# Dense work of the third of four attention layers: a smaller budget per sub-step and a lower bar for a second piece

## The chip, the cores and the metric

The kernel runs on one core of a Trainium2 chip. A core has a matrix engine (TensorE, PE in the profile), whose weight loads are listed apart (PEld), a vector engine (VectorE, DVE), an engine for activations and copies (ScalarE, ACT), a general one (GpSimd, POOL), and a queue engine that here only issues transfers (SyncE, SP). The metric is the device time of one execution in microseconds (us); lower is better. The median of three executions of the kernel before is 1722.2 us (1716.13 to 1724.42).

## The reference

The input x has 8 batches of 256 tokens with 512 features, and there is a context of the same shape. Four cross-attention layers follow each other; each reads the output of the one before and the same context:

```python
x = layer1(x, ctx, mask)        # layer norm, 16 heads of 32, output projection, then an MLP 512 -> 2048 -> 512
x = layer2(x, ctx)              # one head of width 512: x + alpha * softmax(q k^T / sqrt(512)) v w_o
x = layer3(x, ctx, mask2)       # 32 query heads of 16 share 8 key/value heads; then layer norm
x = layer4(x, ctx, mask)        # 16 heads of 32 on the layer-normed context; x + tanh(gate) * out
```

For the third layer:

```python
scores = einsum('bkgld,bksd->bkgls', q, k) * scale + mask2   # per batch: 32 heads, 256 x 256
out    = einsum('bkgls,bksd->bkgld', softmax(scores), v) @ Wo + bo
y      = layer_norm(out + x) * gamma + beta
```

Everything is float32. The kernel reaches that accuracy by splitting a matrix into a rounded part ("hi") and a rest ("lo") and multiplying three times (hi hi, hi lo, lo hi), so a projection takes three times the matmuls that it would take once.

## The kernel before

**Stages.** First the attention of layer 1 with its own pipeline, then its MLP, then one pipeline (called at L1639) over 64 units: units 0 to 31 are layer 3, unit number 4b + ft for batch b and a quarter ft of the heads, and units 32 to 63 are layer 4. In the trace of before, layer 3's part runs from about 825 to 1416 us and layer 4's to the end.

**A tick.** Tick t of the pipeline has four sub-steps (chunks), written t.0 to t.3 here. In each, the attention of two units is issued first: A (L1277, scores of unit t with queries in rows, two matmuls; L1287, four VectorE instructions that add the mask and take the row maxima) and C (L1330, scores of unit t - 2 transposed, two matmuls; then L1340 copy on ScalarE and L1341 mask on GpSimd for the one half, L1343 on VectorE for the other, and L1345 the exponential on ScalarE). Once per tick come B (L1308 to L1311: the maxima of unit t - 1 are transposed and put, by a transfer, into the operand that C will use) and the product of probabilities and values, AV (L640), of the unit that has just ended C. AV's result goes through memory (avd, L1370 to L1375) and is divided in E (L1383 to L1388).

**The dense work as filler.** Everything else of layers 2 to 4 is written as generators that a class `Fillers` (L283) holds in a queue. After A and C of a sub-step the pipeline calls `tick(us, budget)` (L304). It adds the budget to an account, held to at most 8, and lets the generators advance piece by piece while the account is above zero; each piece takes its estimated time from it. So the account may go below zero by a large piece, and is filled again by the budgets that follow. For layer 3 the budget per sub-step is a quarter of B2 = 9.0, that is 2.25 (a quarter of 10 in the first three ticks); for layer 4 B3 = 5.5 holds.

**Who is next.** `one()` (L315) goes on first with a tile that is half done. Then it takes the first entry of the queue that has not run yet in this sub-step. An entry that has run may give a second piece only if the account is above 1.4:

```python
for again in (False, True):
    for e in self.q:
        if e[1] <= self.now and (not self.even or again and self.acc > 1.4 or e not in self.ran):
```

The entries are `l2_post` (L1544, ahead of the others), `l12_fill` (L1397: layer 2's attention and layer 3's queries, batch after batch) and `context_fill` (L1468: what is made of the context). `until()` (L339) forces pieces without regard to the account where the attention needs a result, and sets the account to zero.

**The pieces of a batch**, with the letters used below and the estimates that the account is charged:

| letter | piece | matmul line, tile | estimate, us |
|---|---|---|---|
| S | half a tile of the context times layer 2's key matrix (`scores_side` L1122) | L213 cx,ws | 1.28 |
| K | keys of layer 3 | L213 cx,ws | 1.28 |
| V | values of layer 3 | L227 ws,cx | 1.28 |
| R | half a tile of the context times layer 2's value matrix (`rows` L1165) | L227 ws,cx | 1.28 |
| X | layer 1's output transposed, two per batch (`features` L1185) | L1185 | 0.85 |
| s | half of layer 2's scores; behind the second the softmax, L1206 and L1207 on VectorE and L1211 twice on ScalarE | L1196 | 1.71 |
| T | transposes of those probabilities, copied by L1234 on ScalarE | L1228 | 0.85 |
| o | half of layer 2's output | L1241 | 1.71 |
| F | that output transposed, two per batch; copied out by L391 and its neighbours | L383 | 0.85 |
| Q | half of layer 3's queries | L213 x,wq | 1.28 |
| P | half a tile of the projection behind the attention (`l2_post`) | L227 wo,at | 1.28 |

A batch holds 18 of 1.28, four of 1.707 and five of 0.853, 34.1 in all.

**Order.** In ticks 2 to 25 the program order of TensorE is written out by hand (`keep_order` L776): A and C of a sub-step, then the sub-step's pieces; B and AV stand behind the first sub-step's pieces. From unit 26 on, the framework's scheduler sets the order. Transfers are issued by SyncE in one queue.

**Buffers.** The weights that S, K, V and R need come in through three slots `ws`: two for layer 2's key matrix (`med`), one for K and V (`wkvd`), and layer 2's value matrix (`mnd`, two loads of 1 MB issued where the last S ends) into the two slots that S has freed. The raw context of a batch is split into halves (L179 on ScalarE, L180 on GpSimd) some time ahead of the first S.

Of the kernel before, what the change touches and what calls it, by code (L numbers as in the profile page):

```python
# [20 lines left out]
PASSES = ((0, 0), (0, 1), (1, 0))  # L21
MMUS = 1.0 / 2400.0
B0, B0E = 6.2, 9.0
B2, B3 = 9.0, 5.5
LEAD = 5
N3, NFA = 0, 5
PRIO = 100
# [49 lines left out]
def tile_xattn_stack(  # L77
# [205 lines left out]
    class Fillers:  # L283
# [29 lines left out]
        def one(self):  # L313
            if self.open:
                self.adv(self.open)  # L315
                return True

            for again in (False, True):
                for e in self.q:
                    if e[1] <= self.now and (not self.even or again and self.acc > 1.4 or e not in self.ran):  # L320
                        self.ran.append(e)
                        self.adv(e)
                        return True
            return False
# [1255 lines left out]
    kst = [ph5.T([P, 4, 256], R, "ks") for _ in range(2)]  # L1580
    one = const.tile([4, 256], F, name="one")
    nc.gpsimd.memset(one, 1.0)
    for t in kst:
        nc.gpsimd.memset(fp(t), 0.0)
# [162 lines left out]
```

## Time and profile before

| quantity | value |
|---|---|
| median of three executions (range) | 1722.2 us (1716.13 to 1724.42) |
| the profiled execution, its time | 1719.88 us |
| its span, first to last instruction | 1718.1 us |
| mean granted TensorE clock | 0.968 of full speed |
| instructions | 28352 |
| moved by transfers | 329.16 MB, mean 192 GB/s |
| duration of ticks 16 to 19, one batch (1103.3 to 1167.5 us) | 64.2 us |

All durations below are from that one execution. A line of the page's group list names the source line, the engine, the operation, the output tile, an arrow and the input tiles, the shape, and how often; then busy time, the mean of one in ns, and the idle time of the engine ahead of the group with what ended most of it. A line of the waits reads: engine, waiting instruction, arrow, what released it; total idle time, how often, the longest. "Issue" is time in which nothing that the profile shows held the engine back. A line in order of time gives the start, the duration, the engine, the instruction, and in brackets the idle time ahead of it. The stretches give, between two times, the busy time of each engine, the mean granted clock of TensorE (PEclk; 1.00 is full speed), the share of time in which the transfer engines were busy, and GB/s.

### The profile page before, as it was taken

To read this page: it belongs to the slowest core of one execution; us is meant where nothing else is said; L and a number is where in the kernel's file an instruction comes from. 1 tells how busy PE (TensorE), PEld (TensorE's weight loads), DVE (VectorE), ACT (ScalarE), POOL (GpSimd) and SP (SyncE) were. 2 spreads that over 40 slices of the span, in tenths; PEclk is the share of its full clock that TensorE was granted. 3 is DMA by queue.
4 is the path that set the end of the run, shared out by engine and by line. 5 is a ranking of instruction groups with operands and counts; after the bars stand their busy time and mean duration, and the time that the engine had idled before them with its cause. 6 is when DMAs were issued, how large, how long until landed. Compare 5 with 4: busy or idle time off the path is not lost.

```text
span 1718.1 us, 28352 instructions
## 1 busy us (share of the span) xinstructions
PE 1591.8 (93%) x9984; PEld 1222.5 (71%) x9984; DVE 1071.7 (62%) x2380; ACT 875.8 (51%) x1563; POOL 774.5 (45%) x792
## 2 busy tenths in 40 slices
PE   6999999999989999999798899999988998999998
PEld 5877866777658778887576577677565876777765
DVE  7248556777756867643466578678777775654343
ACT  5226445555455565553255466565564564444454
POOL 6336234323474675532135456557556575222111
PEclk9999999999999999999899999999988999999999
DMA  8969677454542443356755575585366676766552
GB/s 290 306 225 304 205 234 229 153 167 130 179 159 81 151 131 126 120 188 217 238 186 199 168 272 178 192 278 170 107 192 187 200 224 201 231 215 212 179 164 74
DMA packets 169308, 329.16 MB, mean 192 GB/s; under 512 B 17200, under 2 KB 85200, under 8 KB 163664
## 3 DMA queue, kind: packets, MB, share of 16 engines
q1 hardware_dynamic: 169168, 327.36, 58.9%
q8 instruction: 80, 1.31, 0.3%
q14 instruction: 60, 0.49, 0.1%
HBM read 230.79 MB, written 96.49 MB: 190 GB/s over the span
## 4 chain that ended last, share of the span: by engine, by line
PE 60%; DMA 14%; DVE 10%; POOL 5%; issue 4%; ACT 3%; SPq 3%; DVEq 0%; POOLq 0%; ACTq 0%
PE pp L213 20%; PE pp L227 19%; PE av L640 7%; PE sm L1277 3%; PE sm L685 3%; PE st L721 3%; PE st L1330 2%; DVE sm L1287 2%; PE pp L1196 1%; PE pp L1241 1%; DMA h<-in_ctxn_dram 1%; PE pp L383 1%; DMA ws<-mnd 1%; DMA stack<-q0d 1%; POOL fw L180 1%
## 5 line engine op out<-in xcount | busy, mean ns | idle before, releaser
L692 DVE TENSOR_REDUCE negm<-sm 128x2 f32<-128x512 f32 x256 | 168.9, 682 | 126.1 <-PE sm L685 125.7
L729 ACT ACTIVATE P<-st 128x512 f32<-128x512 f32 x256 | 145.2, 594 | 125.3 <-PE st L721 118.3
L213 PE MATMUL pp<-ys,fw 128*128 128x512 f32 x768 | 190.2, 397 | 7.7 <-ACT fw L179 4.4
L227 PE MATMUL pp<-pw,gs 128*128 128x512 f32 x768 | 191.7, 396 | 2.9 <-ACT gs L1031 2.6
L213 PEld LDWEIGHTS pp<-ys,fw 128*128 128x128 f32 x768 | 143.2, 190 | 41.7 <-ACT fw L179 4.6
L640 PE MATMUL av<-P,V 128*32 128x256 f32 (+1 forms) x2204 | 168.8, 406 | 4.1 <-DVE xt L754 3.1
L227 PEld LDWEIGHTS pp<-pw,gs 128*128 128x128 f32 x768 | 141.1, 188 | 37.9 <-ACT gs L1031 3.7
L213 PE MATMUL pp<-x,wq 128*128 128x256 f32 x1152 | 159.4, 286 | 7.1 <-DVE x L391 2.2
L213 PEld LDWEIGHTS pp<-x,wq 128*128 128x128 f32 x1152 | 148.7, 190 | 16.6 <-DVE x L391 3.6
L1287 DVE CUSTOM_DVE_ANT_0 sm<-sm,va 128x256 f32<-128x256 f32 x256 | 103.6, 443 | 47.4 <-PE sm L1277 47.1
L1287 DVE CUSTOM_DVE_ANT_0 sm<-sm,vb 128x256 f32<-128x256 f32 x256 | 103.5, 442 | 47.2 <-PE sm L1277 46.9
L1032 POOL TENSOR_TENSOR gs<-xt,gs 128x512 fp32r<-128x512 f32 x64 | 91.9, 1443 | 85.6 <-ACT gs L1031 85.6
L1277 PE MATMUL sm<-ks,stack 96*128 96x512 f32 x256 | 100.3, 458 | 23.0 <-DVE mx L1287 12.6
L227 PE MATMUL pp<-wo,at 128*128 128x512 f32 x384 | 105.5, 408 | 4.5 <-POOL at L1387 1.7
L640 PEld LDWEIGHTS av<-P,V 128*32 128x32 f32 x2204 | 62.0, 110 | 60.0 <-issue 21.1
L1027 DVE SCALAR_TENSOR_TENSOR xt<-xt,xt 128x512 f32<-128x512 f32 x64 | 67.9, 1064 | 58.5 <-ACT xt L1026 58.5
L1345 ACT ACTIVATE P<-P 128x1024 f32<-128x1024 f32 x77 | 81.4, 1059 | 41.9 <-POOL P L1341 36.1
L180 POOL TENSOR_TENSOR fw<-stg,fw 128x1024 fp32r<-128x1024 f32 x32 | 82.2, 2578 | 34.5 <-ACT fw L179 19.5
L1277 PEld LDWEIGHTS sm<-ks,stack 96*128 96x128 f32 x256 | 46.8, 199 | 64.8 <-issue 52.8
L227 PEld LDWEIGHTS pp<-wo,at 128*128 128x128 f32 x384 | 70.2, 192 | 27.3 <-issue 3.3
L1330 PE MATMUL st<-stack,ks 100*128 100x512 f32 x256 | 87.2, 411 | 2.3 <-DVE P L1343 1.3
L697 POOL CAST mhl<-negm 128x8 fp32r<-128x8 f32 x64 | 16.1, 251 | 156.6 <-DVE negm L692 156.4
(215 smaller groups left out, 3613.5 us busy)
## 6 DMA issues: line engine op xcount, KB each, us to landing
stg<-in_wfc_dram SPq DMA_DIRECT2D x32, 512.0 KB
stg<-in_wpr_dram SPq DMA_DIRECT2D x32, 512.0 KB
ws<-med SPq DMA_DIRECT2D x16, 1024.0 KB
ws<-mnd SPq DMA_DIRECT2D x16, 1024.0 KB
q2d<-nat SPq DMA_DIRECT2D x48, 256.0 KB
stack<-q2d SPq DMA_DIRECT2D x32, 384.0 KB
k0d<-nat SPq DMA_DIRECT2D x16, 512.0 KB
stack<-k0d SPq DMA_DIRECT2D x32, 256.0 KB
```

The lines of the kernel that those rows point to most:

```text
L180: lo.tensor_tensor(w[:, 1], stg, fp(w[:, 0]), ALU.subtract)
L213: nc.tensor.matmul(pt[:, :n], lhsT=sel(ws, wj, kc)[:, ft * P : (ft + 1) * P], rhs=sel(xs, xj, kc), start=(k == 0), stop=(k == 11),)
L227: nc.tensor.matmul(pt[:, :n], lhsT=sel(xs, xj, kc)[:, tt * P : (tt + 1) * P], rhs=sel(ws, wj, kc), start=(k == 0), stop=(k == 11),)
L640: self.prev = nc.tensor.matmul(o, lhsT=lhsT, rhs=rhs, start=start, stop=stop, skip_group_check=True).ins
L692: nc.vector.tensor_reduce(self.negm[:, 2 * h : 2 * h + 2], pt.rearrange("p (q k) -> p q k", q=2), AX.X, ALU.max, negate=True)
L729: nc.scalar.activation(p, pt, AF.Exp)
L1027: nc.vector.scalar_tensor_tensor(v, v, 1.0 / GA, u, ALU.add, ALU.mult)
L1032: nc.gpsimd.tensor_tensor(lo, u, fp(hi), ALU.subtract)
L1277: nc.tensor.matmul(pts[qt], lhsT=self.qs[0:96, h, qt * P : (qt + 1) * P], rhs=self.ks[0:96].rearrange("p u k -> p (u k)"), start=True, sto ...
L1287: nc.vector.tensor_tensor_reduce(out=t, in0=t, in1=self.am[:, qt, :], scale=1.0, scalar=-3.0e38, op0=ALU.add, op1=ALU.max, accum_out=self. ...
L1330: nc.tensor.matmul(pt, lhsT=self.ks[0:100, u, kt * P : (kt + 1) * P], rhs=self.qs[0:100, 2 * hp : 2 * hp + 2, :].rearrange("p h t -> p (h ...
L1345: last["act"] = nc.scalar.activation(pf, pf, AF.Exp).ins
```

## The change

Two constants change. B2 falls from 9.0 to 8.6: the budget of a sub-step from 2.25 to 2.15, and of a batch's sixteen sub-steps from 36.0 to 34.4, against the 34.1 that a batch's pieces are charged. The bar for a second piece of the same entry in one sub-step falls from 1.4 to 0.9. The bar holds from the last stretch of the MLP on, B2 for units 3 to 31.

```diff
-B2, B3 = 9.0, 5.5
+B2, B3 = 8.6, 5.5
...
-                    if e[1] <= self.now and (not self.even or again and self.acc > 1.4 or e not in self.ran):
+                    if e[1] <= self.now and (not self.even or again and self.acc > 0.9 or e not in self.ran):
```

No instruction is added or taken away. What moves is the sub-step that a piece stands in. In a batch in the steady part (ticks 16 to 19; four sub-steps of a tick between bars):

| tick | before | after |
|---|---|---|
| 16 | T S, S, o S, S o | P P, s, s, T o |
| 17 | F, F K, Q Q, Q Q | o, F F, Q Q, Q Q |
| 18 | V, R R, R R, none | S S, S, S K, V |
| 19 | X, X s s, P P, P P | X R R, X R, R, P P |

So the sub-step 18.3 of each batch, without a piece before, has one after; 4.3 is empty in both. In tick 4 after, s and T of batch 1 stand together in 4.1. The first S of batch 3 moves from 5.2 to 6.0. In the tail, 25.1 to 26.0 were empty and now 26.0 to 26.3 are; before unit 32 starts, `until()` now forces five pieces of layer 4's dense work at once (two halves of a query or key projection, two of values, one transpose), and one small piece at 38.3. From unit 39 on the order of all engines is the same.

## The prediction

> **What bounds the kernel now.** I read the page first, then the stretches of the third layer, then TensorE's waits there, and at last single stretches in order of time.
>
> ```profile
> PE 1591.8 (93%) x9984; PEld 1222.5 (71%) x9984; DVE 1071.7 (62%) x2380; ACT 875.8 (51%) x1563; POOL 774.5 (45%) x792
> ...
> PE 60%; DMA 14%; DVE 10%; POOL 5%; issue 4%; ACT 3%; SPq 3%; DVEq 0%; POOLq 0%; ACTq 0%
> ```
>
> TensorE (PE) is busy 93% of the span and carries 60% of the chain that ended last. The change moves work on PE and adds none, so only PE's idle time, and the pace at which it runs, can change. Unit 3 chunk 3 to unit 26 (890.8 to 1270.0 us) is the part whose order changes most; "busy time by stretch" shows it whole, then one steady batch, then four short stretches of low granted clock:
>
> ```profile
> core 0: us, PE busy (x) PEld busy (x) DVE busy (x) ACT busy (x) POOL busy (x), PEclk, DMA share, GB/s
> 890.80:1270.00 379.20, 348.01 (x1962) 252.65 (x1961) 272.03 (x962) 217.86 (x381) 211.65 (x211) 0.97 0.59 198
> 1103.30:1167.50 64.20, 60.73 (x358) 44.99 (x356) 48.90 (x177) 38.81 (x68) 39.10 (x40) 1.00 0.65 217
> ...
> 1215.00:1225.00 10.00, 8.31 (x37) 4.06 (x36) 5.02 (x19) 4.89 (x8) 3.21 (x3) 0.66 0.14 45
> 975.00:985.00 10.00, 7.73 (x21) 4.34 (x20) 7.47 (x23) 4.83 (x11) 8.64 (x8) 0.66 0.30 105
> 921.00:926.00 5.00, 3.60 (x14) 3.31 (x15) 0.52 (x2) 1.89 (x5) 4.32 (x5) 0.67 0.46 157
> 1085.00:1089.00 4.00, 3.01 (x20) 1.22 (x22) 2.55 (x11) 3.11 (x5) 1.64 (x2) 0.69 0.86 285
> ```
>
> PE is idle 31.2 us of 379.2, and runs slow in four places. The waits of PE in that stretch, by what ended them:
>
> ```profile
> PE sm L1277 <- issue: 5.0, 4, 1.2
> ...
> PE av L640 <- ACT pk L1345: 2.3, 2, 1.3
> PE pp L227 <- DMA ws<-mnd: 2.1, 1, 2.1
> ```
>
> And PE in order of time about the empty sub-step 18.3 of the steady batch:
>
> ```profile
> 1147.29 0.64 PE L1277 MATMUL sm<-ks,stack 96*128 96x512 f32 x2
> 1147.77 0.63 PE L1330 MATMUL st<-stack,ks 100*128 100x512 f32 x2
> 1149.65 0.90 PE L1277 MATMUL sm<-ks,stack 96*128 96x512 f32 x2 [1.25 <-issue]
> ```
>
> With no dense piece the sub-step still takes 2.36 us, because VectorE (DVE) needs that long for its four L1287 and one L1343; PE has 0.94 us of work in it. The AV matmuls behind then wait another 0.98 us for the exponentials.
>
> **The change, part by part.** Pieces are renamed in nothing and counted the same; only their sub-steps change (the table of the change's section). Costs and gains are summed over 890.8 to 1270.0, five changed batches and a half.
>
> What goes: (1) the empty sub-step. The "issue" rows are 5.0 us in four, the AV waits behind them 2.3 and 1.0; 4.3 stays empty, so 8.3 - 1.25 = 7.0. What is late next there is nothing on DVE's side: every other sub-step holds more than DVE's 2.4 us, but for the one with two F (below). (2) The waits for a context's halves (ScalarE 2.0, GpSimd 2.0): batch 3's first S moves from 5.2 to 6.0; I take 2.5, as the halving still stands only two sub-steps ahead. (3) The post matmuls start one sub-step later, and their waits for GpSimd (1.7 and 0.7) go: 2.0. (4) PE's 1.9 us for L1211 at 975.6, replaced below. (5) Pace: the steady batch takes 64.2 us; at the clean rates of its own rows (16 x 0.94 for A and C, 4 x 2.06 for B and AV, 35.0 of dense work) it is 58.3. Idle is 3.5 of the 5.9 between, 2.4 are matmuls that wait inside their rows; I let half of that go, 1.2 x 5 = 6.0. (6) The four low-clock stretches lose 3.4 + 3.4 + 1.65 + 1.2 = 9.7 us of PE's pace, each after a gap that now goes; PE fills eight tenths of them: 8.0. Sum: 27.4 us.
>
> What comes: (1) In the new order T, the transposes of the L1 probabilities, stands one A and C behind the last s, where before two post pieces lay between. The chain it waits for is in the trace, in the same order on DVE:
>
> ```profile
> 1159.76 0.69 DVE L1206 TENSOR_REDUCE sm<-pp 128x2 f32<-128x512 f32 x1 [2.52 <-PE pp L1196]
> ...
> 1161.69 0.98 DVE L1207 TENSOR_SCALAR sm<-sm 128x2 f32<-128x2 f32 x1
> 1162.71 0.47 ACT L1211 ACTIVATE p<-pp,sm 128x256 f32<-128x256 f32 x1 [1.43 <-DVE sm L1207]
> ...
> 1163.18 0.46 ACT L1211 ACTIVATE p<-pp,sm 128x256 f32<-128x256 f32 x1
> ```
>
> From 1159.76 to 1163.64 it is 3.9 us, because two L1287 and an L1343 stand between L1206 and L1207; with 0.1 to reach PE and 0.94 of A and C beside it, PE stands 3.0 us. PE's order is fixed here, so behind T wait o, the next A, C and AV, and with them DVE and ACT. Five times (units 8, 12, 16, 20, 24, chunk 3): 15.0. In 4.1 T stands right behind s, but L1207 right behind L1206: 1.9 us, as 895.4 to 897.3 in the trace. Together 16.9. (2) o stands directly behind T and needs its copy: a T row of 0.60, L1234 of 0.59 and about 0.25 to reach PE, less the 0.45 that T itself takes: 1.0 x 5 = 5.0. (3) R comes 6.6 to 6.9 us behind the last S, which frees the buffer that mnd is loaded into; before it was 20 us in the steady batches. The one near case is the wait of 2.1 us above: SyncE issued that load at 937.26 and R ran at 947.77, 10.5 us for about 3.1 MB in flight. Now about 2.6 MB are: at the 350 GB/s that the half-microseconds before that landing moved 7.4, with the landing about 8.1, so 1.2 us of wait x 5, less the 2.1 that it replaces: +3.9. Bounds: none of it (-2.1) or 10.5 - 6.9 = 3.6 each (+16). The two loads now also stand on SyncE's queue behind the nd loads, which wait for the avd store; that lies in the bound. (4) F F in one sub-step and Q directly behind: Q's second matmul needs L391, 0.65 x 5 = 3.3 (0 to 5). (5) Clock: of the seven places here where PE's gaps add up to 1.9 us or more, five were followed by a clock of about 0.67. With 3.0 and 1.0 us gaps, 0.7 x 5 dips at 1.9 us each: 7.0 (0 to 17). (6) What I can't name, 0.4 per batch: 2.0 (0 to 10). Sum: 38.1 us.
>
> The tail (units 26 to 31 and the fourth layer's start): four sub-steps stay empty (26.0 to 26.3, before 25.1 to 26.0), the budget is 0.1 smaller, and five pieces of fourth-layer work are forced at once before unit 31. They are PE work that is owed anyway, but the last value weights are loaded right before: +2 (-4 to +7). From unit 39 the order is as before: nothing, for it is the same work in the same order.
>
> Sum: 1719.9 (the profiled execution; its span is 1718.1) - 27.4 + 38.1 + 2 = 1732.6. That execution lies 2.3 us under the median of 1722.2, so I forecast a median of **1735 us**, slower by 0.7%.
>
> Two rules speak against two of these prices, and nothing above needs them. The Trainium skill, "TensorE: Matmul & The Clock Gate", Part 1, says that the clock falls after a whole idle window of about 3.4 us; by that the gaps of 3.0 and 1.0 us might never lower it and the sum would be 1725.6, but in this trace 0.66 follows a gap of 1.9 us. "DMA: Bandwidth & Descriptors", Anatomy of one DMA, gives 2.0 us plus the bytes at 436 GB/s, an estimate of 4.4 us for 1 MB, and R would never wait (sum 1726.6); the trace has 10.5.
>
> **The rivals.** *Not slower: T waits short.* If DVE is so far ahead that L1207 runs 1.9 us behind s, as in 4.1, T costs 1.0 instead of 3.0 (-10.2) and such gaps leave the clock alone (-7): 1715, as a median 1718. It decides when the T wait is under about 1.5 us. Against it: the three instructions stand between in all five batches, and the four steady rows of this chain agree within 0.1 us. *Faster: evenness.* If besides the whole 2.4 us of lost pace goes, with the 5.9 us of waits for L1287 and some of the low clock in units 26 to 31 (0.85 in 1270 to 1340): 1718 - 6 - 5 - 6 = 1701. For it: half the loss of the first changed batch (77 us against 64) is waits that the new order does not have. *Much slower: the transfer bounds.* mnd late by 3.6 each time and a dip behind every gap: +12 and +10, 1757. For it: the DMA share is 0.65 in the steady batch. *The change does nothing:* excluded; in the order as built no sub-step of units 5 to 25 is empty.
>
> **How the numbers follow.** Forecast 0.42 (1735), T short 0.25 (1718), evenness 0.20 (1701), transfer 0.13 (1757). About 0.5% (8.6 us, under 1713.6 or over 1730.8) is what a measurement here can tell. Faster: evenness and a little of T short, 0.23. Same: most of T short and the low edge of the forecast, 0.26. Slower: the rest, 0.51. Range 1706 to 1755: it takes in most of evenness, and all but the end of the transfer case. The forecast's own is 1726 to 1745.
>
> **What would show it.** Right: PE L1228 <- ACT p L1211 at about 15 us in five, L1241 waiting for L1234 about 1 us each; PE L1277 <- issue down to about one time; low clock behind unit 8, 12, 16, 20 and 24 chunk 3; some wait for mnd. Wrong: T waits under 1.5 us, or the first changed batch gaining over 15 us, or gaps of 3 us at full clock. It would also be wrong if the forced run before unit 31 leaves PE waiting for weights.

## The result, and the profile after

The changed kernel takes 1747.2 us (median of six, 1744.5 to 1751.9), the kernel before 1722.6 us (median of six, 1716.1 to 1726.4). The ratio is 1.015, with a 95% interval of 1.013 to 1.018: slower by 1.5%, about twice what was forecast.

The profiled execution of the changed kernel took 1751.93 us (span 1750.2; the slowest of its six), that of the kernel before 1719.88. Of these 32.1 us of span, 10.2 lie ahead of sub-step 4.0, where the order is the same. In sixteen profiles taken in this study that sub-step starts at 890.8 to 902.5 us, and the kernel before has the earliest start of all. So this part is scatter between executions, and I compare from sub-step 4.0 on. From there to the second score matmul of 26.0, called 4.0 to 26.0 below, is the stretch that the prediction showed for the kernel before (it began it at "unit 3 chunk 3", one sub-step too early in name). It went from 379.2 to 401.8 us, +22.6; from there to the end it is 448.1 and 447.4, no change.

From the page of the changed kernel, the busy times and the chain that ended last:

```profile
PE 1614.8 (92%) x9984; PEld 1231.7 (70%) x9984; DVE 1081.5 (62%) x2380; ACT 879.4 (50%) x1563; POOL 776.2 (44%) x792
...
PE 65%; DMA 14%; DVE 10%; issue 4%; POOL 3%; ACT 3%; SPq 2%; DVEq 0%; ACTq 0%; POOLq 0%
```

TensorE does the same 9984 matmuls and is busy 23 us longer (1591.8 before). Matmuls that take longer without more work mean a lower clock, or waits inside the rows. The stretches say which; the first is 4.0 to 26.0, the second one batch (12.0 to 16.0), the others are places of low clock in it and in two later batches:

```profile
core 0: us, PE busy (x) PEld busy (x) DVE busy (x) ACT busy (x) POOL busy (x), PEclk, DMA share, GB/s
901.00:1302.80 401.80, 363.37 (x1947) 256.77 (x1947) 280.52 (x962) 216.91 (x377) 210.75 (x210) 0.94 0.55 180
...
1041.50:1112.80 71.30, 65.15 (x358) 46.15 (x358) 51.70 (x175) 39.49 (x68) 38.79 (x39) 0.95 0.58 192
1058.00:1066.00 8.00, 6.51 (x13) 3.47 (x14) 3.76 (x13) 2.68 (x7) 2.42 (x4) 0.57 0.51 164
...
1134.00:1141.00 7.00, 6.44 (x10) 3.40 (x11) 2.62 (x9) 2.05 (x3) 0.25 (x1) 0.52 0.34 114
1205.00:1213.00 8.00, 5.95 (x12) 3.03 (x13) 3.10 (x11) 2.88 (x7) 1.77 (x3) 0.57 0.49 161
```

The granted clock falls to 0.57 or less over 7 to 8 us at a time, and 4.0 to 26.0 has 0.94 where the kernel before had 0.97. Cut into stretches of 1 us, with one minus the granted clock added up, the time lost to the clock there is 25.6 us against 13.2: +12.4. PE's idle time (length less busy) is 38.4 against 31.2: +7.2. These two are 19.6 of the 22.6 us. The other 3.0 are rows that take longer without a lower clock: TensorE's busy time, each moment weighed with its granted clock, went from 337.3 to 340.3 us. What ended PE's idle time in 4.0 to 26.0 of the changed kernel (the prediction showed the rows of before):

```profile
PE pp L1228 <- ACT p L1211: 14.1, 6, 2.6
PE sm L1277 <- DVE mx L1287: 13.7, 16, 1.2
PE pp L1241 <- ACT nat L1234: 3.4, 5, 0.7
PE pp L227 <- POOL at L1387: 3.3, 5, 2.1
PE sm L1277 <- issue: 1.2, 1, 1.2
PE pp L227 <- DMA ws<-mnd: 0.9, 2, 0.5
```

The empty sub-steps are gone (issue 5.0 to 1.2, and AV's waits 3.3 to 0.7), T waits as forecast, and one row has grown that the prediction did not price: the scores waiting for VectorE's L1287, 5.9 before and 13.7 now. The row of before:

```profile
PE sm L1277 <- DVE mx L1287: 5.9, 8, 1.1
```

PE in order of time through 12.2 and 12.3 shows both, and the clock:

```profile
1051.30 0.47 PE L1277 MATMUL sm<-ks,stack 96*128 96x512 f32 x1 [1.06 <-DVE mx L1287]
1052.93 0.47 PE L1277 MATMUL sm<-ks,stack 96*128 96x512 f32 x1 [1.16 <-DVE mx L1287]
...
1053.71 1.89 PE L1196 MATMUL pp<-ec,x 128*128 128x256 f32 x8
1055.25 0.82 PE L1277 MATMUL sm<-ks,stack 96*128 96x512 f32 x2
1055.91 0.63 PE L1330 MATMUL st<-stack,ks 100*128 100x512 f32 x2
1058.81 1.36 PE L1228 MATMUL pp<-ident,p 128*128 128x128 f32 x4 [2.27 <-ACT p L1211]
1060.84 3.78 PE L1241 MATMUL pp<-ec,nat 128*128 128x512 f32 x4 [0.68 <-ACT nat L1234]
1063.64 1.84 PE L1277 MATMUL sm<-ks,stack 96*128 96x512 f32 x2
```

T waits 2.27 us for the probabilities. From then on everything takes twice as long: T 1.36 us instead of 0.60, A's two matmuls 1.84 instead of about 0.8. In half-microsecond stretches the clock is at 0.50 from 1058.8 to 1065.7 us. Before T, two waits of 1.06 and 1.16 us for L1287 stand in 12.2, with no T near. VectorE and GpSimd in order of time show where they come from:

```profile
1048.57 0.69 DVE L1343 TENSOR_TENSOR pk<-st,va 128x512 f32<-128x512 f32 x1
1049.18 1.57 DVE L367 TENSOR_SCALAR h<-h,sm,sm 128x512 f32<-128x512 f32 x1
1049.20 1.27 POOL L1341 TENSOR_TENSOR pk<-pk,va 128x512 f32<-128x512 f32 x1 [0.99 <-ACT pk L1340]
...
1050.67 0.42 DVE L1287 CUSTOM_DVE_ANT_0 sm<-sm,vb 128x256 f32<-128x256 f32 x1
1050.83 1.27 POOL L1553 TENSOR_TENSOR h<-h,bc 128x512 f32<-128x512 f32 x1 [0.36 <-DVE h L367]
...
1051.02 1.37 DVE L367 TENSOR_SCALAR h<-h,sm,sm 128x512 f32<-128x512 f32 x1
1052.31 0.42 DVE L1287 CUSTOM_DVE_ANT_0 sm<-sm,vb 128x256 f32<-128x256 f32 x1
```

L367 is the last step of layer 3's layer norm behind the two P. In the new order P P stands in 12.0 and the two s, alone, in 12.1 and 12.2. A sub-step with one s is about 2.6 us of TensorE work (2.57 and 2.66 in e14_cured below, where nothing holds it back), and VectorE needs nearly that for L1287 and L1343; two L367 of 1.57 and 1.37 us do not fit. In the steady batches before, the sub-steps behind the two P held T S and S, and L367 took a third of the time:

```profile
1172.37 0.73 POOL L365 TENSOR_TENSOR sm<-sm,mhalf 128x2 f32<-128x2 f32 x1
...
1173.13 1.00 DVE L367 TENSOR_SCALAR h<-h,sm,sm 128x512 f32<-128x512 f32 x2 [1.31 <-POOL sm L365]
```

Two of them in 1.00 us. So there are two suspects: T right behind s, and the layer norm beside the two s.

### The profile page after: what moved, and what is told of

Same layout as the page of the kernel before. It is cut to its first block, busy times and chain, and to the rows that moved or that the text cites. A ratio compares the mean times of both kernels' runs of the same rounds, so it can differ in the third digit from the quotient of the medians.

```text
span 1750.2 us, 28365 instructions
## 1 busy us (share of the span) xinstructions
PE 1614.8 (92%) x9984; PEld 1231.7 (70%) x9984; DVE 1081.5 (62%) x2380; ACT 879.4 (50%) x1563; POOL 776.2 (44%) x792
## 4 chain that ended last, share of the span: by engine, by line
PE 65%; DMA 14%; DVE 10%; issue 4%; POOL 3%; ACT 3%; SPq 2%; DVEq 0%; ACTq 0%; POOLq 0%
PE pp L213 20%; PE pp L227 20%; PE av L640 8%; PE sm L1277 3%; PE st L721 3%; PE sm L685 3%; PE st L1330 2%; DMA ws<-mnd 2%; PE pp L1241 2%; DVE sm L1287 2%; PE pp L1196 1%; DVE h L367 1%; DMA q3d<-nat 1%; PE pp L383 1%; DMA hl<-hd 1%
## 5 line engine op out<-in xcount | busy, mean ns | idle before, releaser
L1287 DVE CUSTOM_DVE_ANT_0 sm<-sm,vb 128x256 f32<-128x256 f32 x256 | 104.3, 440 | 55.5 <-PE sm L1277 55.0
L1287 DVE CUSTOM_DVE_ANT_0 sm<-sm,va 128x256 f32<-128x256 f32 x256 | 103.6, 443 | 56.3 <-PE sm L1277 56.1
L1277 PE MATMUL sm<-ks,stack 96*128 96x512 f32 x256 | 105.4, 475 | 27.0 <-DVE mx L1287 21.6
L1277 PEld LDWEIGHTS sm<-ks,stack 96*128 96x128 f32 x256 | 47.3, 201 | 72.9 <-issue 57.9
L180 POOL TENSOR_TENSOR fw<-stg,fw 128x1024 fp32r<-128x1024 f32 x32 | 81.7, 2563 | 34.4 <-ACT fw L179 19.4
L697 POOL CAST mhl<-negm 128x8 fp32r<-128x8 f32 x64 | 16.3, 254 | 177.6 <-DVE negm L692 177.4
```

The costliest lines, as they stand in the source:

```text
L180: lo.tensor_tensor(w[:, 1], stg, fp(w[:, 0]), ALU.subtract)
L1277: nc.tensor.matmul(pts[qt], lhsT=self.qs[0:96, h, qt * P : (qt + 1) * P], rhs=self.ks[0:96].rearrange("p u k -> p (u k)"), start=True, sto ...
L1287: nc.vector.tensor_tensor_reduce(out=t, in0=t, in1=self.am[:, qt, :], scale=1.0, scalar=-3.0e38, op0=ALU.add, op1=ALU.max, accum_out=self. ...
```

## The experiments

In all tables and texts "stretch" is 4.0 to 26.0, from the one profile of each kernel; medians and ratios are of all runs, each against the kernel before on the same chip (its medians there are 1724.6 to 1725.8 us).

| kernel | median, us | ratio (95% interval) | profiled execution | stretch | T waits for L1211 | L1277 waits for L1287 | lost to the clock |
|---|---|---|---|---|---|---|---|
| before | 1722.6 | 1 | 1719.9 | 379.2 | 1.9 | 5.9 | 13.2 |
| changed | 1747.2 | 1.015 (1.013 to 1.018) | 1751.9 | 401.8 | 14.1 | 13.7 | 25.6 |
| e1_budget | 1803.2 | 1.044 (1.041 to 1.047) | 1803.1 | 451.0 | 14.3 | 16.3 | 44.4 |
| e2_bar | 1717.7 | 0.995 (0.992 to 0.998) | 1719.8 | 370.8 | 1.9 | 6.9 | 5.6 |
| e3_cut | 1717.1 | 0.996 (0.994 to 0.998) | 1721.5 | 373.7 | none | 13.8 | 8.5 |
| e4_noln | 1727.4 | 1.002 (1.000 to 1.004) | 1729.2 | 384.8 | 15.4 | 2.6 | 17.1 |
| e5_fold | 1731.7 | 1.003 (1.001 to 1.005) | 1744.7 | 392.6 | 7.4 | 13.7 | 20.5 |
| e6_both | 1713.2 | 0.991 (0.988 to 0.995) | 1713.2 | 360.8 | none | 2.6 | 1.7 |
| e7_88 | 1730.2 | 1.003 (1.001 to 1.005) | 1729.9 | 385.4 | 9.4 | 4.2 | 12.0 |
| e10_barfold | 1715.6 | 0.995 (0.992 to 0.997) | 1724.0 | 373.2 | none | 8.1 | 10.2 |
| e11_lead | 1729.2 | 1.002 (1.000 to 1.004) | 1735.2 | 379.7 | 2.2 | 11.2 | 8.5 |
| e12_bboth | 1723.7 | 1.000 (0.998 to 1.002) | 1722.1 | 381.0 | none | 4.3 | 14.0 |
| e13_halve | 1804.6 | 1.047 (1.044 to 1.050) | 1802.2 | 451.6 | 14.3 | 16.3 | 46.1 |
| e14_cured | 1715.3 | 0.994 (0.991 to 0.997) | 1705.8 | 367.4 | 7.5 | 2.6 | 5.1 |
| e15_bcured | 1716.5 | 0.995 (0.993 to 0.997) | 1721.2 | 374.9 | none | 5.7 | 11.9 |
| e16_lnact | 1730.1 | 1.001 (0.998 to 1.004) | 1732.8 | 380.7 | 13.6 | 2.6 | 15.4 |

One profile is one execution, and not always a typical one: e5_fold's is the slowest of ten, e14_cured's the fastest of nine. So comparisons of whole times go by the medians. For the clock the record has every execution's mean grant. One minus that grant, times the span, averaged over a kernel's executions, is for the whole kernel 69 us with the change and 59 to 62 before it; it is 53 for e3_cut, 60 for e4_noln, 58 for e5_fold, 63 for e16_lnact, 51 for e6_both and 55 for e14_cured.

### The two parts of the change apart

e1_budget has only the smaller budget:

```diff
-B2, B3 = 9.0, 5.5
+B2, B3 = 8.6, 5.5
```

> The budget alone (B2 = 8.6, bar still 1.4). No sub-step from 5.0 to 25.3 is empty here either, and T still stands one A and C behind the last s (T alone in 16.3, both o in 17.0, then F, F S S, Q Q, Q Q, S, S K, V). Theory 1 (the wait of T for the probabilities, about 2.3 us, and the half clock of about 3.4 us lost behind it, in each of five batches, carry the loss): these stay, only o no longer waits for the copy (0.68 us x 5 = 3.4), so about 1743 us. Theory 2 (the loss is spread over the layout, above all the bar's Q, S and R in pairs): much of it goes, about 1730 us. If the cost lay in the bar alone: 1722 us.

Measured: 1803 us, 78 more than before; every theory missed it. T's waits are the same 14.3 us, but a new row leads PE's waits in the stretch:

```profile
PE pp L213 <- ACT cx L179: 26.7, 5, 5.3
...
PE pp L1228 <- ACT p L1211: 14.3, 6, 2.6
PE pp L227 <- DMA ws<-mnd: 9.2, 5, 2.5
```

With the old bar of 1.4 a batch has "F, F S S, Q Q, Q Q": S comes as the second entry in the sub-step and finds the context not yet split (L179), 5.3 us in each of five batches, each followed by half clock. With the bar at 0.9 the second F and the Q go first, and S comes later.

e2_bar has only the lower bar:

```diff
-                    if e[1] <= self.now and (not self.even or again and self.acc > 1.4 or e not in self.ran):
+                    if e[1] <= self.now and (not self.even or again and self.acc > 0.9 or e not in self.ran):
```

> The bar alone (0.9, B2 still 9.0). The steady batch is that of before but for one X and one S, with T two P behind the last s and an empty sub-step. All theories: the same as before, 1722 us within 5; if it is slower by 10 us or more, the second pieces themselves cost something that no theory has.

Measured: 1717.7 us, ratio 0.995: within the 5 us expected, and a small gain. So the budget costs and the bar takes most of it back: +78 alone, -7 alone, +25 together. The two parts do not add.

### The two suspects, by leaving work out

e3_cut lets T read another tile, so that nothing of it waits for the softmax:

```diff
                     nc.tensor.transpose(
                         tp[:, kt * 256 + qt * P : kt * 256 + (qt + 1) * P],
-                        self.p1[:, qt, kt * P : (kt + 1) * P],
+                        self.hs[qt][:, kt * P : (kt + 1) * P],
                         ident,
                     )
```

> The changed kernel, with the transposes T reading the layer's input instead of the probabilities: T no longer waits for the softmax of layer 2; layer 2's result is left out by that, all instructions stay. Theory 1: the 14.1 us of waits in six places go, and with them the half clock behind T in five batches (5 x 3.3 = 16), so 1747 - 30 = 1717 us. Rival (the clock falls whatever T does, because of the L1287 waits before it): only 14 us go, 1733 us. Rival 2 (what T waited for becomes a wait of the next matmuls): 1740 us or more.

Measured: 1717.1 us, as theory 1 has it; that it fits to the microsecond is luck, for the eight executions lie between 1712.6 and 1721.5. The stretch loses 28.1 us, of which 17.1 are the clock. One wait for L1211 is left there, 2.25 us ahead of a matmul of another piece.

e4_noln leaves the layer norm out:

```diff
-        ys = layer_norm_tiles(ph5, hb, 1e-6)
+        ys = list(hb)
```

> The changed kernel without the layer norm of layer 3 (L361, L362, L364, L365 and L367 are left out; the multiplications by gamma and beta stay). It stands on VectorE while the sub-steps with one s each run. Theory 1: the L1287 waits of 2.2 us a batch go (11 us) but T's waits and the half clock behind them stay: 1736 us. Rival (the layer norm holds VectorE back, and so also delays L1206 and L1207 and starts the clock's fall): the waits, T's waits in part (5 us) and the dips at units 16, 20 and 24 chunk 1 (8 us) go too: 1720 us.

Measured: 1727.4 us, between the two. The L1287 waits go (13.7 to 2.6) and 8.5 us of clock with them, but T's waits do not shorten (15.4). So the layer norm is a cause of its own, and not the reason for T's wait.

e6_both makes both cuts.

> The changed kernel with both cuts at once: T reads the layer's input (layer 2's result is left out) and layer 3's layer norm is left out. If the two causes were independent, their gains add: 28.1 + 17.0 us in the stretch of units 4 to 25, so about 1700 us, under the kernel before. If they share the clock's falls (each alone takes some of the same falls away), 1706 to 1712 us. All clock loss in that stretch should be under 4 us.

Measured: 1713.2 us, just above the 1706 to 1712 expected for shared falls, with 1.7 us lost to the clock. The gains in the stretch are 28.1 and 17.0 alone and 41.0 together, so 4 us are shared. Two stretches, e3_cut's and e6_both's:

```profile
898.80:1272.50 373.70, 347.58 (x1947) 251.16 (x1946) 278.00 (x962) 216.05 (x377) 210.56 (x211) 0.98 0.59 194
```

```profile
902.50:1263.30 360.80, 338.85 (x1947) 245.96 (x1946) 258.04 (x932) 215.36 (x377) 206.04 (x201) 1.00 0.62 201
```

With both gone the clock is at full speed in all but 3.4 of 361 us, and PE is busy 24.5 us less than in the changed kernel for the same matmuls.

e12_bboth makes the same two cuts in the kernel before.

> The kernel before with the same two cuts as e6_both (T reads the layer's input, layer 3's layer norm is left out). Beside e6_both it shows what the even spread alone is worth once neither cause can act. If the prediction's gains (empty sub-step 7.0, halves 2.5, pace 6.0 and some clock) were real, units 4 to 25 take about 370 us here against 360.8 in e6_both, and the whole about 1715 us. If the even spread is worth nothing: about 361 us there, 1705 us.

Measured: 1723.7 us, no gain at all (1.000); both numbers missed. The kernel before does not suffer from these two causes. Against it e6_both is 10.5 us faster: this is what the even spread is worth by itself. The stretch of e12_bboth, beside e6_both's above:

```profile
895.30:1276.30 381.00, 349.95 (x1965) 255.91 (x1963) 265.67 (x935) 218.71 (x382) 207.60 (x202) 0.96 0.59 198
```

e6_both has less idle time (21.9 against 31.0 us) and loses less to the clock (1.7 against 14.0). The clock part is one execution's: in the five kernels with about the order of before (before, e2_bar, e10_barfold, e12_bboth, e15_bcured) it is anything from 5.6 to 14.0.

### The two suspects, with all work kept

e5_fold takes L1207 out of the chain, by putting its factor into a copy:

```diff
-            nc.scalar.copy(self.es[:, 2 * i : 2 * i + 2], pt.rearrange("p (k t) -> p k t", k=2))
+            nc.scalar.activation(
+                self.es[:, 2 * i : 2 * i + 2], pt.rearrange("p (k t) -> p k t", k=2), AF.Identity, scale=1.0 / 512.0**0.5
+            )
...
-            nc.vector.tensor_scalar(nb, nb, sc, None, ALU.mult)
...
                     bias=nb[:, qt : qt + 1],
-                    scale=sc,
```

> The changed kernel with layer 2's factor 1/sqrt(512) put into the copy that S makes anyway, so that L1207 goes and the exponential starts behind L1206; the arithmetic is the same but for rounding. The chain behind the last s falls from 3.6 us to about 2.1. Theory 1 (T's wait and the half clock behind it): T waits about 0.8 us instead of 2.3, that is 7 us less in five batches, and if that is short enough for the clock, up to 5 dips of 1.7 us fewer: 1732 to 1740 us. Rival (the VectorE jam by the layer norm sets the clock's fall and T only follows): 7 us at most, 1740 us.

Measured: 1731.7 us, at the lower end. T's waits halve (14.1 to 7.4). The clock's loss is 5.1 us lower in the one profile, and 11 us lower for the whole kernel on the mean of all executions (69 to 58).

e16_lnact moves L367 to ScalarE, with two small GpSimd instructions that make its bias:

```diff
+        if act:
+            nm = ph.T([P, n], F, "sm1")
+            nc.gpsimd.tensor_tensor(nm, mv[:, :, 0], rs, ALU.mult)
+            nc.gpsimd.tensor_scalar(nm, nm, -1.0, None, ALU.mult)
         for i, t in enumerate(tiles):
-            nc.vector.tensor_scalar(t, t, mv[:, i, 0:1], rs[:, i : i + 1], ALU.subtract, ALU.mult)
+            if act:
+                nc.scalar.activation(t, t, AF.Identity, bias=nm[:, i : i + 1], scale=rs[:, i : i + 1])
+            else:
+                nc.vector.tensor_scalar(t, t, mv[:, i, 0:1], rs[:, i : i + 1], ALU.subtract, ALU.mult)
...
-        ys = layer_norm_tiles(ph5, hb, 1e-6)
+        ys = layer_norm_tiles(ph5, hb, 1e-6, act=True)
```

> The changed kernel with only the last step of layer 3's layer norm (L367) on ScalarE, nothing left out; beside e5_fold (only the shorter chain, 1732) and e14_cured (both, 1715) it gives the two repairs apart. In the changed kernel's trace each of these L367 takes 1.37 to 1.58 us and ends 0.28 us behind a GpSimd addition that runs beside it; in the kernel before's steady batches, where none runs beside it, 0.54 us. If that is the second cause, the L1287 waits in units 4 to 25 fall from 13.7 to under 5 us and the two sub-steps with one s each take 2.6 us, as in e14_cured; T's waits (14 us) stay: 1724 to 1732 us. If the layer norm's place only matters together with the chain: 1740 us or more.

Measured: 1730.1 us. The L1287 waits fall to 2.6 us, T's stay at 13.6: the second cause is real with all work kept.

e14_cured has both repairs.

> The changed kernel with both causes lessened by real means, nothing left out: the factor in S's copy (as in e5_fold) and the last step of layer 3's layer norm (L367, two of about 1.4 us a batch on VectorE) done on ScalarE. If the two causes found by leaving work out carry the loss, it lands between e5_fold (1732) and e6_both (1713): 1714 to 1722 us, with the L1287 waits in units 4 to 25 down from 13.7 to under 6 us and at most 10 us of clock loss. If the layer norm only shifted the wait (to ScalarE, which also does the exponentials): 1728 us or more.

Measured: 1715.3 us, ratio 0.994 (0.991 to 0.997), faster than both kernels. The repairs are worth 15.5 and 17.1 us alone and 31.9 together, by the medians (the kernel before ran 2 to 3 us slower beside the repaired kernels than beside the changed one). PE in order of time through 16.1 to 16.3 (the lines are shifted: L1284 is L1277, L1205 is L1196, L1235 is L1228, L1248 is L1241):

```profile
1099.93 1.89 PE L1205 MATMUL pp<-ec,x 128*128 128x256 f32 x8
1101.47 0.82 PE L1284 MATMUL sm<-ks,stack 96*128 96x512 f32 x2
...
1102.59 1.89 PE L1205 MATMUL pp<-ec,x 128*128 128x256 f32 x8
1104.13 0.81 PE L1284 MATMUL sm<-ks,stack 96*128 96x512 f32 x2
...
1105.86 0.33 PE L1235 MATMUL pp<-ident,p 128*128 128x128 f32 x1 [0.45 <-ACT p L1219]
1106.81 0.55 PE L1235 MATMUL pp<-ident,p 128*128 128x128 f32 x3 [0.61 <-ACT p L1219]
1108.64 1.98 PE L1248 MATMUL pp<-ec,nat 128*128 128x512 f32 x4 [1.29 <-ACT nat L1241]
```

No wait for VectorE, T waits 1.06 us in two pieces, o 1.29, and the four o matmuls take 1.98 us instead of 3.78: the clock has not fallen here. In this profile, the fastest execution, it falls twice in 4.0 to 26.0; nine times in the changed kernel's.

### Other orders

e7_88 is the new bar with B2 = 8.8:

```diff
-B2, B3 = 9.0, 5.5
+B2, B3 = 8.8, 5.5
```

> The new bar of 0.9 with B2 = 8.8: in the layout as built the last s stands two P ahead of T in units 16 to 23, and the sub-steps are as even as in the changed kernel but for one empty one in tick 22. Theory 1 (T's place and the layer norm's beside the light sub-steps carry the loss, not the even spread as such): 1712 to 1722 us. Rival (the smaller budget itself delays what layer 4 needs): 1735 us or more.

Measured: 1730.2 us; both numbers missed. The first batches keep T right behind s (9.4 us of waits in three places, up to 4.4), and one B waits 3.9 us for VectorE's L1301. The expectation looked at the steady batches alone.

e11_lead is the changed kernel with LEAD = 6, which puts both s ahead of the two P:

```diff
-LEAD = 5
+LEAD = 6
```

> Both parts of the change, and LEAD = 6 instead of 5, so that layer 2's scores of the next batch may start one tick earlier. In the layout as built both s stand ahead of the two P, T two P and two A and C behind the last s, and beside the layer norm stand T R and R; one sub-step of a batch is empty. Nothing is left out. Theory (the loss is where T and the layer norm stand, not the even spread or the smaller budget): T's waits under 3 us in all and clock loss under 8 us in units 4 to 25, so 1710 to 1720 us. Rival (the smaller budget and the lower bar cost by themselves): 1735 us or more.

Measured: 1729.2 us; the waits of T came out as expected (2.2), the time did not. The layer norm now stands beside T R and R and holds L1287 back there (11.2 us), the empty sub-step is back (issue 7.5 us), and Q directly behind F waits for L390 and L391 (4.6). The place of the light sub-step changed, not that the layer norm meets one.

e10_barfold is e2_bar with the shorter chain, e15_bcured that with the layer norm on ScalarE too (diffs as above).

> The bar alone (0.9, B2 = 9.0) with the factor put into S's copy, as a version that may beat the kernel before. With two P between s and T, T waits little there already (1717.7 us with the bar alone): the shorter chain takes at most the waits that are left, 2 to 4 us: 1713 to 1717 us. Had the chain no part in it: 1718 us.

> The bar alone with the same two repairs, as the version that may be fastest. Its T stands two P behind s and its layer norm beside two S, so there is little left to cure: 1711 to 1716 us, against 1715.6 of e10_barfold. If ScalarE, which is nearer to TensorE's needs here, becomes late: 1720 us or more.

Measured: 1715.6 us, and 1716.5 us with a ratio of 0.995 (0.993 to 0.997). Neither can be told from e2_bar's 1717.7: where the two causes do not act, the repairs bring nothing.

e13_halve was to show where e1_budget's waits come from:

```diff
-CLAG, WLAG = 9.0, 6.0
+CLAG, WLAG = 7.0, 6.0
```

> The budget alone (e1_budget, 1803 us) with the context halved two units of the planner's time earlier (CLAG = 7.0 instead of 9.0); TensorE's order stays as in e1_budget. If its 78 us come from S standing right behind the halving (26.7 us of waits for ScalarE and the half clock behind, 5 us in each of five batches), most of that goes: 1755 to 1770 us. If S waits for something else that shows up as ScalarE: 1795 us or more.

Measured: 1804.6 us, no change. In its trace the split of the context (L179) stands on ScalarE where it stood, behind an exponential that waits for GpSimd, and TensorE still waits 5.33 us for it: the edit did not move it. What an earlier split would bring stays open.

## Why the prediction was right or wrong

The sign and the main wait were right, the size was half. By its steps, in 4.0 to 26.0:

**The waits for T** (cost 1): forecast 16.9, measured 14.1 in the same six places, 2.1 to 2.6 each in the five where 3.0 was taken. **o behind T** (cost 2): 5.0 forecast, 3.4 measured, five times 0.68. Right in mechanism and nearly in size.

**The clock** (cost 5 and gain 6) is the step that failed. The prediction let four low-clock stretches go (8.0) and gave the new gaps 0.7 falls of 1.9 us per batch (7.0, range 0 to 17), a net of -1.0. Measured: 25.6 us lost in the changed kernel in place of 13.2, +12.4. At T's wait the clock fell in all five batches, each time for 6.8 us at half clock, which loses 3.4: 17.1 in all, already the end of the range. It fell once for 3.4 us behind T's wait in 4.1 (1.7), and in three batches once more ahead of T, behind the waits for L1287 (6.8). A fall was priced at 1.9 us where most cost 3.4, the falls behind L1287 were not foreseen, and of the losses that went the prediction had not read the one from 1264.0 us on. e3_cut, e6_both and e14_cured show the term by its absence.

**What was not named** (cost 6, 2.0): the layer norm behind P, 7.8 us more of waits for L1287 and part of the clock. The prediction said that nothing on VectorE would be late where the empty sub-step was filled. It put this term at nothing because it looked at VectorE's 2.4 us per sub-step of attention and not at what else moves beside the light ones. e4_noln and e16_lnact show it: 20 and 17 us less.

**The gains**: the empty sub-steps gave 6.4 of 7.0 (issue 3.8, AV 2.6); the waits for a context's halves 4.0 of 2.5. The post matmuls' wait for GpSimd did not go (2.0 forecast): it is 3.3 now, 2.4 before. The pace (6.0) did not come: TensorE's busy time weighed with the clock rose by 3.0 us. In e6_both it is 337.1 against 337.9 in e12_bboth, so the 10.5 us that the even spread is worth once nothing stands in its way are idle time and clock, not pace. This is the second step that failed, by 9 us. One wait of 2.7 us for the transfer of h2d ahead of F, which the prediction did not count, went too.

**Rows waiting for mnd** (cost 3): +3.9 forecast, 0.9 measured in place of 2.1, so -1.2. R starts 6.9 us behind the issue of the first load, as forecast, and in all five batches finds it there, which the prediction had at 8.1. Its second half waited twice, 0.42 and 0.47 us, for the second load, 7.7 and 8.3 us behind that one's issue. One slow load in the trace of before was no price for five. That R would never wait was the estimate by the Trainium skill's "DMA: Bandwidth & Descriptors" (Anatomy of one DMA), 4.4 us for 1 MB; the page gives this fit for transfers that GpSimd issues, these are SyncE's, and the two waits do not agree with it.

**F F and Q** (cost 4): 3.3 forecast for Q waiting for L391; no such wait shows. In its place L1277 waits 0.42 to 0.44 us for L1287 there, five times, 2.1, which is part of the 13.7. **The tail**: +2 forecast, -0.7 measured (447.4 against 448.1), with the pieces forced before unit 32 costing nothing visible.

**The rivals.** "T waits short" (1718) did not come: T waits 2.1 to 2.6 us, and e5_fold and e14_cured show what it would have been worth. "Evenness" (1701) is what the changed order does when both causes are cut away, 1713. "The transfer bounds" (1757) lies about as far from 1747 as the forecast; of its two parts the falls of the clock behind the gaps came, the late transfer did not.

## What to carry to other kernels

When work is spread evenly, look at each engine in the sub-steps that become lighter: what bursts beside them (here a layer norm on VectorE) can hold back the next sub-step although that engine is only 70% busy in the stretch (280.5 of 401.8 us). Price a wait of TensorE with the clock that it may cost behind it: here 14.1 us of waits for T cost 30 in all (1747.2 to 1717.1). Add up the idle time that falls within a few microseconds: short gaps close together counted here like one long gap (next section). And when two constants are tuned together, measure each alone; here one cost 78 us and the other hid most of it.

## What the runs showed of the hardware

**The clock falls in windows of time.** Every loss in 4.0 to 26.0 of the changed kernel is 1.7 or 3.4 us, that is 3.4 or 6.8 us at a clock of 0.50; the fall at 1058.8 us lasted until 1065.7. In each of the sixteen traces all falls in this stretch begin whole multiples of 3.413 us after the first, to about 1 ns. The Trainium skill, "TensorE: Matmul & The Clock Gate", Part 1, names a window of about 3.4 us that runs freely, which agrees with these steps. It also lets the clock fall after an idle window; here less was enough. Cut by these steps, the sixteen stretches have 1670 windows that ran at full clock. Of the 69 in which TensorE idled 1.80 us or more, every one was followed by a fall; of the 1510 with less than 1.25 us, none; of the 91 between, 29. (The ends of TensorE's rows are modelled in the profile, so the two bounds are rough.) The two gaps of 1.06 and 1.16 us for L1287 thus count together where one window holds both, or most of both: so in three batches, with a fall ahead of T, and not in two. In e6_both o waits 8.3 us in five places, up to 1.7 at once, and only one fall shows in the stretch. Where a window happens to begin decides such cases, which fits the spread between executions of one kernel.

**VectorE's L367 waits for GpSimd.** In both traces its median is about 0.54 us, and in the stretch, where a two-input GpSimd instruction is running already or starts with it, it ends behind the end of that: in each changed batch one takes 1.57 us beside L1341 and one 1.37 beside L1553, ending 0.28 us behind them; the longest in the whole traces take 2.6 to 3.1. Of the changed kernel's eight L367 in units 12 to 24 all are so drawn out (1.37 to 1.58); of the four in the steady batches before, none (0.54 to 0.55). There L1553 starts 0.16 us behind the second L367 and is itself the longer one, 1.52 us instead of 1.27. The Trainium skill, "VectorE: DVE Perf Modes", in the section "Two Vector instructions with no wait between them", speaks of a second read interface that VectorE shares with GpSimd, used by an instruction with one input in its two-port mode. That would be the reason; no run here tried another form of the instruction. L1207, which the prediction counted with 0.98 us, ran beside such an addition too (GpSimd's L1341 from 1161.36 to 1162.65); with no GpSimd instruction beside it, it takes 0.16 to 0.17.
